# A convolution, attention and recurrence network on one core: the norm of the next image inside the last attention block, and a feed-forward in more steps

## The chip, the cores and the metric

The kernel runs on one core of one Trainium2 chip. Its metric is the device time of one execution in microseconds, given as the median of several runs. The engines that matter are TensorE (matmuls and transposes, PE in the profile, with PEld for its weight loads), VectorE (DVE), ScalarE (ACT), GpSimd (POOL), and SyncE (SP), which issues most of the transfers. Each engine works through its own queue in order.

## The reference, cut to what matters

The input is x of shape (4, 128, 64, 64): four images of 128 channels and 4096 positions. What is computed, in short:

```python
# layer 0
g = groupnorm(x, 32 groups)
e1, e2, asm = prelu(1x1 conv of g)            # 64, 64, 128 channels
x = x + softmax(e1^T e2) @ asm                # 4096 x 4096 scores per image
# layer 1, on tokens t (4096 x 128 per image)
a = layernorm(t)
q = running products of cos(a + rx)           # 16 heads of 8
a1 = layernorm(a + attention(q, q, q) @ w_comb.T + b_comb) * g1 + beta1
h  = relu((cos(a1[..., :8]) * cos(ry)) @ w1.T + b1)      # 512 wide
t  = t + layernorm(a1 + h @ w2.T + b2) * g2 + beta2
# last step, over all images
wx = batchnorm(layernorm(t) @ W.T)
y_t = sigmoid(wx_t + y_(t-1) @ V.T)           # along the positions
out = t + y
```

Here norms with no factors of their own are meant where none are written, and a1 is added again before the last norm of the attention layer.

## The kernel before, in words

The four images pass through two stages each. The first stage (`first_stage`, `layer0`) is the convolution attention: two convolutions of the normed image give e1 and e2 in four pieces of 1024 positions (`both_convs`, lines 373 to 387), a third gives asm, and then for each of eight chunks of 512 columns sixteen blocks of scores are multiplied on TensorE (`scores`, L439), exponentiated on ScalarE (L443), summed on VectorE (L451) and weighed on TensorE (L458). The second stage (`second_stage`, `attention`) is the attention over 16 heads, taken as eight pairs of heads with four blocks each. A block is a list of units (`order`, line 891). A unit multiplies scores (L948), exponentiates them (L960) and is weighed two units later (L801). Scores are symmetric, so "other" units, which lie off the diagonal, are also turned by VectorE (`run_flips`, L767) and multiplied a second time for the mirrored side (`mirror_step`, L780), sixteen steps for four units, into halves of one PSUM bank (`misc`); VectorE adds them up (L794). "Own" units on the diagonal need no turning. A last block has twelve other and four own units, in the order three other, one own. In the very last block of an image the exponentials go to a pool of six tiles, two for each unit, because the buffer of the image (`xs`) that otherwise serves as well is being loaded with the next image.

That load and the statistics of the next image's group norm are a generator (`prepare_image`, `norm_stats`, lines 333 and 1398). It is advanced once at the first unit of the last block and once at each of the units 6 to 13: one load and eight pieces of statistics (L337). The rest, two tiny matmuls (L342, L351) into the PSUM slot called `ps_tok` and a power on GpSimd (L241), is run after the last turning of the block. Then the next first stage begins with four of the eight normalisations (L363) and its convolutions.

The feed-forward of an image (`feed_forward`, line 1053) is done in eight groups of 512 tokens, and runs interleaved with the first stage of the next image; that of the fourth image runs alone at the end (`third_stage`). It is a generator too, with pauses (`yield`) between its steps. In the first stage `meanwhile` calls `step_late` once or twice after every weighed block, from the ninth call on; each call advances every living group by one step, and `in_steps(..., 14, 2)` starts a new group each 14 steps with at most two alive. The order of TensorE, ScalarE and VectorE in these stages follows the order in which the code issues the work; in `third_stage` a scheduler orders it. The steps that matter here: the projection of the attention (L1075), v and its statistics, the norm v on ScalarE (L283), the product with g1 and the sum with fb2 on GpSimd (L1083, L1084), the cosine, the 512 hidden values (L1120, L1129), the product back (L1137), u with its statistics and norm, the product with g2 and the sum with be2 on GpSimd (L1152, L1153), t2 on VectorE (L1158), its transposes (L291) and copy, its norm, transposes again, a copy to `last` (L1237), and the matmul for the batch norm's statistics (L1178, L1179). Matmuls of the feed-forward take turns on two PSUM banks (`ps_one`).

Of the kernel before, what the change touches and what calls it, by code (L numbers as in the profile page):

```python
# [26 lines left out]
def kernel(  # L27
# [32 lines left out]
    P = 128  # L60
# [19 lines left out]
    stats = ctx.enter_context(tc.tile_pool(name="stats", bufs=4))  # L80
# [252 lines left out]
    def norm_stats(n, xs):  # L333

        st = once.tile([P, NIC, 6], F32, tag="gst", name=f"gst{n}")
        for i in range(NIC):
            nc.vector.bn_stats(st[:, i, :], xs[:, ts(i, IC)])  # L337
            yield
        mv = once.tile([P, 2], F32, tag="gmv", name=f"gmv{n}")
        nc.vector.bn_aggr(mv, st)  # L340
        pg = get("ps_tok", f"pg{n}")
        nc.tensor.matmul(pg[:, 0:1], grp, mv[:, 0:1], start=True, stop=True)  # L342
# [5 lines left out]
        nc.vector.scalar_tensor_tensor(tv, dm, dm, mv[:, 1:2], ALU.mult, ALU.add)  # L348
        yield
        pv = get("ps_tok", f"pv{n}")  # L350
        nc.tensor.matmul(pv[:, 0:1], grp, tv, start=True, stop=True)  # L351
        yield gm, rsqrt(pv[:, 0:1], 1e-5, [P, 1], f"g{n}")

    def layer0(n, xs, xh, norm, shifted, begin, meanwhile):
# [118 lines left out]
        normalised(0, 4)  # L473
        both_convs(0)
        normalised(4, NIC)
# [164 lines left out]
    def attention(n, q, xs, tail, upcoming):  # L640
# [16 lines left out]
        misc = get("ps_misc", f"misc{n}")  # L657
        turns = []
# [271 lines left out]
        for pair in range(NPAIR):  # L930
            keys, queries, qa, later, denom = ready
            for b in range(NQB):
                block = {"acc": None}
                tiles = order(b)
                end_of_all = pair == NPAIR - 1 and b == NQB - 1

# [3 lines left out]
                for at, unit in enumerate(tiles):  # L940
# [75 lines left out]
                    if end_of_all and (at == 0 or 6 <= at < 6 + NIC):  # L1016
                        next(upcoming, None)
# [35 lines left out]
    def feed_forward(im, i, t2_rows, last, final):  # L1053
# [29 lines left out]
        nc.gpsimd.tensor_tensor(blocks(v), blocks(v), row4(g1_bc), ALU.mult)  # L1083
# [32 lines left out]
        for f0 in range(0, NF, 2):  # L1116
# [10 lines left out]
            for j in range(2):  # L1127
                bias = fb1_sb[:, f0 + j : f0 + j + 1]
                nc.scalar.activation(hs[-1][:, j, :], phs[j], AF.Relu, bias=bias)  # L1129
# [35 lines left out]
        nc.sync.dma_start(out=t2_rows[:, cols], in_=t2T)  # L1165
        norm(u, t2, factors)
# [3 lines left out]
        tokens_i = last(n, i, pt)  # L1170
        yield
# [10 lines left out]
    WsT = const.tile([P, P], F32, tag="WsT", name="WsT")  # L1182

    def fold_norm(W_sb):
# [88 lines left out]
    def first_stage(im, before):  # L1273
# [11 lines left out]
        with stage(f"conv{n}", **pools, **psum), tc.manual_schedule(engines=engines):  # L1285
            own, calls = [], [0]
            step_late = in_steps(feed_forwards(before) if before else [], 14, 2)
# [94 lines left out]
    def hold_every():  # L1382
# [3 lines left out]
        held["W"] = pool.tile([P, P], F32, tag="W_sb", name="W_sb")  # L1386
# [32 lines left out]
    with stage("fold", half=(HALF, 1), ps_one=(ONE, 1)):  # L1419
        fold_norm(held["W"])  # L1420
# [15 lines left out]
    with stage("runs", t2=((P, 2 * IC), 4 * N), half=(HALF, 2 * NS + 2), ps_one=(ONE, 2 * NS)):  # L1436
# [21 lines left out]
        def begin(k, t):  # L1458
# [3 lines left out]
                out_k, WsT, tokens_at(k, t), start=True, stop=t == -WARM, skip_group_check=True  # L1462
# [61 lines left out]
    with tc.If(any_bad > 0):  # L1524
# [5 lines left out]
        with stage(  # L1530
# [7 lines left out]
            W_again = half_tile("W_again")[:, 0:P]  # L1538
            nc.sync.dma_start(out=W_again, in_=W)
            fold_norm(W_again)  # L1540
# [90 lines left out]
```

## Time and profile before

| what | value |
|---|---|
| time before, median of 3 runs | 7238.97 us (7236.84 to 7239.09) |
| profiled execution, its time | 7238.09 us |
| profiled execution, its span | 7236.4 us |
| TensorE busy | 6893.3 us (95%) |
| VectorE busy | 5952.5 us (82%) |
| ScalarE busy | 6007.3 us (83%) |
| GpSimd busy | 2861.6 us (40%) |
| mean granted TensorE clock | 0.976 |

The span is what the profiler saw from the first instruction to the last; the run's own time is a little longer. First stages lie at about 25 to 415, 1665 to 2190, 3440 to 3960 and 5220 to 5740 us of the span, second stages between them, the last feed-forward at about 6982 to 7127 and the recurrence after it. A row of a timeline reads: start, duration, engine, line, operation, tile written <- tiles read, partitions x elements, count, and in brackets the idle time before it with what ended it. A row of waits reads: who waited <- for whom: total us, times, longest. A row of a stretch of time reads: from:to, its length, then the busy time of each engine with its count of instructions, the granted clock, the share of the DMA engines and GB/s.

### The profile page before, as it was taken

The page shows a single profiled execution, that of the slowest core. Times are in us where ns is not written, and L with a number is a line of the kernel's source. Part 1 is how long each engine was busy: PE and PEld are TensorE (multiplying, and loading weights), DVE is VectorE, ACT ScalarE, POOL GpSimd, SP SyncE. Part 2 cuts the span into 40 slices and gives each one's busy share as a digit, 9 for nine tenths or more (in the row PEclk, how much of TensorE's full clock was granted, in tenths as well). Part 3 has the DMA queues.
Part 4 walks back from the last instruction along what each step waited for, and adds up shares of the span by engine and source line. Part 5 has one row for each costly group of instructions (what it writes and reads, how often), then busy time and mean ns, then how long its engine had stood idle before and what let it go on. Part 6 is the DMA issues. An engine that isn't in the chain of part 4 may idle for free. (4 is left out here: it accounts for less than half of the span.)

```text
span 7236.4 us, 224777 instructions
## 1 busy us (share of the span) xinstructions
PE 6893.3 (95%) x92974; PEld 3741.7 (52%) x92974; DVE 5952.5 (82%) x7949; ACT 6007.3 (83%) x11919; POOL 2861.6 (40%) x10021
## 2 busy tenths in 40 slices
PE   8999999998989999999988999999998899999977
PEld 4545555555554555554554455555455455555546
DVE  5678899887768899889676998888867788898984
ACT  4479999995558999999455999999855599999976
POOL 0024444434323454443433354444433244444542
PEclk9999999999999999999998999999999999999988
DMA  1010000001111000000111100000011100000012
GB/s 38 30 39 25 29 20 21 21 9 35 38 43 40 27 22 20 22 23 20 30 38 44 37 22 20 21 25 21 23 32 36 44 33 22 22 26 27 11 60 106
DMA packets 85393, 221.20 MB, mean 31 GB/s; under 512 B 9490, under 2 KB 10644, under 8 KB 83588
## 3 DMA queue, kind: packets, MB, share of 16 engines
q1 hardware_dynamic: 79904, 195.10, 7.9%
q8 instruction: 731, 11.98, 0.7%
q10 hardware_dynamic: 4164, 11.41, 0.4%
q14 instruction: 306, 2.51, 0.1%
q0 software_dynamic: 288, 0.20, 0.0%
HBM read 141.63 MB, written 56.62 MB: 27 GB/s over the span
## 5 line engine op out<-in xcount | busy, mean ns | idle before, releaser
L960 ACT ACTIVATE e<-s 128x1024 f32<-128x1024 f32 (+1 forms) x3480 | 2949.1, 889 | 62.6 <-PE s L948 41.8
L767 DVE STREAM_TRANSPOSE t<-e 128x1024 f32<-128x1024 f32 x2240 | 2587.3, 1208 | 11.4 <-ACT e L960 9.1
L780 PEld LDWEIGHTS misc<-t,mirror 128*32 128x32 f32 x57344 | 1663.6, 110 | 1400.6 <-issue 1348.8
L780 PE MATMUL misc<-t,mirror 128*32 128x128 f32 x57344 | 1994.9, 273 | 20.6 <-DVE later L794 17.7
L960 ACT ACTIVATE xs<-s 128x1024 f32<-128x1024 f32 (+1 forms) x2152 | 1836.4, 894 | 44.6 <-PE s L948 31.5
L767 DVE STREAM_TRANSPOSE t<-xs 128x1024 f32<-128x1024 f32 x1344 | 1558.4, 1208 | 6.6 <-ACT xs L960 5.1
L801 PE MATMUL acc<-e,q_aug 128*32 128x512 f32 x11360 | 1523.7, 608 | 10.8 <-POOL q_aug L683 10.8
L948 PE MATMUL s<-queries,keys 32*128 32x512 f32 x9216 | 1219.7, 497 | 9.4 <-ACT e L960 3.4
L843 POOL COPY own<-o 32x36 f32<-32x36 f32 x2048 | 437.5, 214 | 1710.3 <-DVE o L835 1629.7
L458 PE MATMUL acc<-p,asmT 128*128 128x512 f32 x2048 | 952.5, 597 | 0.0
L801 PE MATMUL acc<-xs,q_aug 128*32 128x512 f32 x7072 | 942.2, 605 | 0.3 <-DVE o L835 0.3
L443 ACT ACTIVATE p<-s 128x1024 f32<-128x1024 f32 x512 | 499.5, 1022 | 468.3 <-PE s L439 452.2
L451 DVE TENSOR_TENSOR total<-total,p 128x1024 f32<-128x1024 f32 x448 | 572.8, 1279 | 326.6 <-ACT p L443 302.9
L948 PEld LDWEIGHTS s<-queries,keys 32*128 32x128 f32 x9216 | 480.2, 182 | 499.4 <-issue 380.0
L737 POOL COPY mirror<-q 32x128 f32<-32x128 f32 x2048 | 602.6, 294 | 237.9 <-PE misc L780 150.2
L868 POOL COPY other<-turned 32x64 f32<-32x64 f32 x1904 | 447.9, 235 | 628.2 <-DVE turned L858 549.6
L439 PE MATMUL s<-hl,e 128*128 128x512 f32 x2048 | 629.3, 452 | 44.9 <-ACT p L443 20.2
L960 ACT ACTIVATION_READ_ACCUMULATOR e<-s 128x1 f32 x2880 | 649.3, 225 | 0.0
L458 PEld LDWEIGHTS acc<-p,asmT 128*128 128x128 f32 x2048 | 386.7, 193 | 341.5 <-issue 317.3
L439 PEld LDWEIGHTS s<-hl,e 128*128 128x128 f32 x2048 | 406.7, 203 | 207.1 <-issue 100.0
L794 DVE TENSOR_TENSOR later<-later,misc 128x128 f32<-128x128 f32 (+1 forms) x576 | 162.7, 282 | 378.5 <-PE misc L780 375.3
L828 POOL COPY by_token<-by_key 32x4 f32<-32x4 f32 x2016 | 390.4, 194 | 85.3
(251 smaller groups left out, 4850.5 us busy)
## 6 DMA issues: line engine op xcount, KB each, us to landing
keys<-parts_dram SPq DMA_DIRECT2D x256, 256.0 KB
queries<-parts_dram SPq DMA_DIRECT2D x1024, 32.0 KB
fx<-x_dram SPq DMA_DIRECT2D x64, 256.0 KB
x_dram<-x SPq DMA_DIRECT2D x56, 256.0 KB
xs<-in_x_dram SPq DMA_DIRECT2D x16, 512.0 KB
t_dram<-t2T SPq DMA_DIRECT2D x32, 256.0 KB
t2s<-t_dram SPq DMA_DIRECT2D x16, 512.0 KB
parts_dram<-high SPq DMA_DIRECT2D x28, 256.0 KB
```

Of the source, the lines that this page charges most:

```text
L439: nc.tensor.matmul(s[:, j, :], stationary, moving, start=y == 0, stop=y == len(parts) - 1)
L443: nc.scalar.activation(p, s, AF.Exp)
L451: nc.vector.tensor_tensor(state[ic], state[ic], p, ALU.add)
L458: nc.tensor.matmul(state["acc", ic], asmT[:, ts(2 * jp + j, P)], p[:, j, :], start=jp == 0 and j == 0, stop=jp == NP - 1 and j == 1,)
L737: nc.gpsimd.tensor_copy(wv[ts(a, 32), s, :, :, ts(a, D)], own[ts(s, 32)])
L767: nc.vector.transpose(group["e"][h][:, k, :], es[h])
L780: nc.tensor.matmul(state["acc"][ts(2 * x + h, 32), :], state["w"][:, QT * (s // 4) + TG * x + s % 4, h, :], state["e"][h][:, :, ds(IC * x ...
L801: nc.tensor.matmul(it["in"]["acc"][ts(2 * h + x, 32), :], it["qa"][:, ds((2 * it["tiles"][x] + h) * V, 32)], it["e"][h][:, ts(x, IC)], sta ...
L843: nc.gpsimd.tensor_copy(own[ts(s, 32), ts(x, 4), h, :], ov[ts(2 * h + x, 32), s, :, 0:V])
L868: copy(to[ts(k, 32), h], tv[ts(2 * x + h, 32), k])
L948: nc.tensor.matmul(ss[h][:, x, :], keys[unit[x] // QT].bitcast(F32R)[r, ts(unit[x] % QT, P)], queries[b].bitcast(F32R)[r, :], start=True, ...
L960: nc.scalar.activation(es[h][:, ts(x, IC)] if split else es[h], ss[h][:, x, :] if split else ss[h].rearrange("p x c -> p (x c)"), AF.Exp, ...
```

## The change

In the last block of an image the order becomes all other units first and the own units last, and the generator of the next image is advanced at the first unit and at each of the last ten, which takes in its last two parts as well. For that the two tiny matmuls of the norm write into spare columns of the bank of the mirrored sums, which are set to zero at the start of the attention (`spare`), without the start flag. The first stage then normalises two pieces ahead of the first convolution and the other six between the first convolution and its activation. The rounding of the lower half of e2 goes from ScalarE to VectorE.

In the feed-forward the products with g1 and g2 go from GpSimd to VectorE, be2 is added to x0 on GpSimd ahead of time (x0's load moves up by two steps), and there are more pauses: between the norm v and the product with g1, before the norm u and after it, between the transposes of t2 and the norm of it, and before the last matmul; one before the product back now holds the addition to x0, one pair before t2 is gone. Three groups may be alive, and the pools follow: x1 from 2 to 3 buffers, fhalf from 6 to 8, stats from 4 to 6, mid from 8 to 7; the folded weights WsT move from the constants into a pool of the last stage.

```diff
-        pg = get("ps_tok", f"pg{n}")
-        nc.tensor.matmul(pg[:, 0:1], grp, mv[:, 0:1], start=True, stop=True)
+        pg = get("ps_norm", f"pg{n}")
+        alone = dict(start=n in (0, "r"), stop=True, skip_group_check=True)
+        nc.tensor.matmul(pg[:, 0:1], grp, mv[:, 0:1], **alone)
...
-        pv = get("ps_tok", f"pv{n}")
-        nc.tensor.matmul(pv[:, 0:1], grp, tv, start=True, stop=True)
+        pv = get("ps_norm", f"pv{n}")
+        nc.tensor.matmul(pv[:, 0:1], grp, tv, **alone)
...
             y, z = mid_tile(f"y{n}_{i}"), mid_tile(f"z{n}_{i}")
+            if i == 0:
+                normalised(2, NIC)
             prelu(pair(e1[:, cols]), pc, y, z, (b12_sb, minus_b12), a12_sb)
-            nc.scalar.copy(pair(e2[CR:P, cols]).bitcast(F32R), pair(e1[CR:P, cols]))
+            nc.vector.tensor_copy(pair(e2[CR:P, cols]).bitcast(F32R), pair(e1[CR:P, cols]))
...
-        normalised(0, 4)
+        normalised(0, 2)
         both_convs(0)
-        normalised(4, NIC)
...
         misc = get("ps_misc", f"misc{n}")
+        spare = [misc[:, ts(k, P)] for k in (2, 3)]
+        for t in spare:
+            nc.vector.memset(t[:, 0:1], 0.0)
+        here["ps_norm"] = lambda name: spare.pop(0)
...
-        def order(b):
+        def order(b, own_last):
...
+            if own_last:
+                return rest + own
             each = len(rest) // TG
             return [u for k in range(TG) for u in rest[each * k : each * (k + 1)] + own[k : k + 1]]
...
-                tiles = order(b)
                 end_of_all = pair == NPAIR - 1 and b == NQB - 1
+                tiles = order(b, end_of_all)
...
-                    if end_of_all and (at == 0 or 6 <= at < 6 + NIC):
+                    if end_of_all and (at == 0 or at >= len(tiles) - NIC - 2):
                         next(upcoming, None)
...
         norm(v, v, factors)
-        nc.gpsimd.tensor_tensor(blocks(v), blocks(v), row4(g1_bc), ALU.mult)
+        yield
+        nc.vector.tensor_tensor(blocks(v), blocks(v), row4(g1_bc), ALU.mult)
         nc.gpsimd.tensor_tensor(blocks(x1), blocks(v), row4(fb2_bc), ALU.add)
...
                 nc.scalar.activation(hs[-1][:, j, :], phs[j], AF.Relu, bias=bias)
+            if f0 == 0:
+                x0 = get("fhalf", f"fx0_{n}_{i}")
+                nc.sync.dma_start(out=x0, in_=im["x0"][:, cols])
             yield
-        yield
-        x0 = get("fhalf", f"fx0_{n}_{i}")
-        nc.sync.dma_start(out=x0, in_=im["x0"][:, cols])
+        nc.gpsimd.tensor_tensor(blocks(x0), blocks(x0), row4(be2_bc), ALU.add)
+        yield
         po = one_psum(f"pf{n}_{i}")
...
         factors = norm_factors(u, "u")
         yield
         yield
+        yield
         norm(u, u, factors)
-        nc.gpsimd.tensor_tensor(blocks(u), blocks(u), row4(g2_bc), ALU.mult)
-        nc.gpsimd.tensor_tensor(blocks(u), blocks(u), row4(be2_bc), ALU.add)
-        yield
-        yield
+        yield
+        nc.vector.tensor_tensor(blocks(u), blocks(u), row4(g2_bc), ALU.mult)
...
         nc.sync.dma_start(out=t2_rows[:, cols], in_=t2T)
+        yield
         norm(u, t2, factors)
         yield
         yield
         pt = transposed(blocks(u), f"pl{n}_{i}")
         tokens_i = last(n, i, pt)
+        yield
         yield
         if n != "r":
             token_products(n, i, tokens_i)
...
-        ffn = dict(x1=(HALF, 2), fhalf=(HALF, 6), hT=(MID, 2))
+        ffn = dict(x1=(HALF, 3), fhalf=(HALF, 8), hT=(MID, 2))
...
-        rest = dict(e=(BIG, 2), big=(BIG, 1), mid=(MID, 8))
+        rest = dict(e=(BIG, 2), big=(BIG, 1), mid=(MID, 7))
...
-            step_late = in_steps(feed_forwards(before) if before else [], 14, 2)
+            step_late = in_steps(feed_forwards(before) if before else [], 14, 3)
```

More of the change, by code (lines that the diff above doesn't have):

```diff
@@ L79 @@
     once = ctx.enter_context(tc.tile_pool(name="once", bufs=1))
-    stats = ctx.enter_context(tc.tile_pool(name="stats", bufs=4))
+    stats = ctx.enter_context(tc.tile_pool(name="stats", bufs=6))
     by_channel = ctx.enter_context(tc.tile_pool(name="by_channel", bufs=1))
@@ L1181, with fold_norm @@
     shift = const.tile([P, 1], F32, tag="shift", name="shift")
-    WsT = const.tile([P, P], F32, tag="WsT", name="WsT")
-    def fold_norm(W_sb):
+    def fold_norm(W_sb, WsT):
         bmv = once.tile([P, 2], F32, tag="bmv", name="bmv")
@@ L1284, in first_stage @@
         engines = {nc.tensor.engine, nc.scalar.engine, nc.vector.engine}
-        with stage(f"conv{n}", **pools, **psum), tc.manual_schedule(engines=engines):
+        others = {"ps_norm": lambda name: get("ps_tok", name)}
+        with stage(f"conv{n}", {}, others, **pools, **psum), tc.manual_schedule(engines=engines):
             own, calls = [], [0]
-            step_late = in_steps(feed_forwards(before) if before else [], 14, 2)
+            step_late = in_steps(feed_forwards(before) if before else [], 14, 3)
             def meanwhile(steps=1):
@@ L1385, in hold_every @@
         held["every"] = pool.tile([P, N, S], F32, tag="every", name="every")
-        held["W"] = pool.tile([P, P], F32, tag="W_sb", name="W_sb")
+        for name in ("W", "WsT"):
+            held[name] = pool.tile([P, P], F32, tag=name, name=f"{name}_sb")
         nc.gpsimd.dma_start(out=held["W"], in_=W)
@@ L1419 @@
     with stage("fold", half=(HALF, 1), ps_one=(ONE, 1)):
-        fold_norm(held["W"])
+        fold_norm(held["W"], held["WsT"])
     WARM, TOL = 16, 1e-6
@@ L1461, in begin @@
             nc.tensor.matmul(
-                out_k, WsT, tokens_at(k, t), start=True, stop=t == -WARM, skip_group_check=True
+                out_k, held["WsT"], tokens_at(k, t), start=True, stop=t == -WARM, skip_group_check=True
             )
@@ L1537 @@
                     token_products(n, i, every[:, n, ts(i, IC)])
-            W_again = half_tile("W_again")[:, 0:P]
+            pool, _ = here["big"]
+            W_again, WsT = (
+                pool.tile([P, P], F32, tag=name, name=f"{name}_again") for name in ("W", "WsT")
+            )
             nc.sync.dma_start(out=W_again, in_=W)
-            fold_norm(W_again)
+            fold_norm(W_again, WsT)
             with tc.For_i(0, S, SC) as s0:
```

## The prediction

> **What bounds the kernel now.** I read the page first (busy shares, slices), then the stretches of 100 us, then the waits of TensorE in one convolution stage, then the timelines at its worst gap and around the change of image.
>
> ```profile
> span 7236.4 us, 224777 instructions
> ...
> PE 6893.3 (95%) x92974; PEld 3741.7 (52%) x92974; DVE 5952.5 (82%) x7949; ACT 6007.3 (83%) x11919; POOL 2861.6 (40%) x10021
> ```
>
> ```profile
> 1900.00:2000.00 100.00, 91.81 (x359) 58.05 (x360) 77.35 (x163) 56.28 (x79) 37.11 (x42) 0.94 0.10 35
> 2000.00:2100.00 100.00, 86.09 (x358) 52.61 (x357) 64.58 (x150) 52.62 (x75) 28.27 (x32) 0.97 0.11 35
> ...
> 2400.00:2500.00 100.00, 99.89 (x1732) 50.45 (x1720) 88.94 (x91) 98.31 (x205) 35.93 (x146) 1.00 0.06 19
> ```
>
> The first is the page, the second the stretches, whose columns are busy us of PE, PEld, DVE, ACT, POOL, then the clock. TensorE sets the time: full in the attention stages (the row from 2400), 86 to 92 of 100 us in the three convolution stages that also carry a feed-forward (1700 to 2200 and its two likes). The five rows of 1700 to 2200 miss 51 us. The waits of TensorE from 1700 to 2215:
>
> ```profile
> PE pt L291 <- DVE t L1158: 14.3, 5, 5.3
> PE pwx L1178 <- ACT last L1237: 7.5, 3, 4.0
> PE acc L801 <- POOL q_aug L683: 5.6, 1, 5.6
> PE s L439 <- ACT p L443: 4.8, 2, 3.6
> PE pc L291 <- ACT hT L1129: 4.2, 7, 0.9
> PE pl L291 <- ACT q L283: 3.0, 1, 3.0
> ```
>
> They are steps of the feed-forward that were issued too close to what they read. At the longest, TensorE stands in front of the transposes of t2 (first line), while VectorE works without a pause and slowly:
>
> ```profile
> 1791.42 1.11 PE L291 MATMUL pt<-ident,t 128*128 128x128 f32 x4 [5.34 <-DVE t L1158]
> ```
>
> ```profile
> 1776.46 4.15 DVE L268 TENSOR_SCALAR x<-x,mv_t,r_t 128x128 f32<-128x128 f32 x4
> 1780.65 1.67 DVE L599 TENSOR_TENSOR arg<-x,rx_bc 128x512 f32<-128x512 f32 x1
> ```
>
> The four normalisations take 4.15 us where their mean of 422 ns makes 1.69, because GpSimd runs five 128x512 operations (L1067, L1083, L1084, L1152, L1153) from 1776.6 to 1783.5. Last, the change of image, TensorE's timeline and one row of VectorE's:
>
> ```profile
> 1662.16 0.38 PE L342 MATMUL pg<-gmv,grp 128*128 128x1 f32 x2 [2.55 <-DVE gmv L340]
> 1663.34 0.35 PE L351 MATMUL pv<-tv,grp 128*128 128x1 f32 x2 [0.79 <-DVE tv L348]
> ...
> 1682.64 3.75 PE L439 MATMUL s<-hl,e 128*128 128x512 f32 x8 [6.40 <-DVE hl L423]
> ```
>
> ```profile
> 1627.25 9.09 DVE L767 STREAM_TRANSPOSE t<-e 128x1024 f32<-128x1024 f32 x8
> ```
>
> The norm of the next image stands after the last block and opens gaps of 2.55 and 0.79 us; the 6.40 us later is the wait for the first scores' operands. Turning a tile costs 9.09 / 8 = 1.14 us.
>
> **What the Trainium skill says.** "SBUF — State Buffer", "Who interferes with whom": a VectorE tensor_tensor with both inputs in SBUF contends with GpSimd's reads, and a tensor_scalar in a two-port mode is shut out for a whole instruction. The trace agrees (4.15 against 1.69 us). "TensorE: Matmul & The Clock Gate", "Why this matters for your kernels": gaps over about 3 us drop the clock. It agrees: after the 5.34 us gap eight score matmuls take 3.76 us, not 2.39, and the next eight of L458 4.08, not 3.59, so that gap costs 1.9 us more. "PSUM — Partial Sum Buffer", "The four PSUM rules": a region set to zero and matmuls without the start flag may share a bank with other groups; so the norm may use the bank of the mirrored sums without a second bank. No row of before shows it; I price the two matmuls as now (0.38 and 0.35 us) and the memsets at under 0.2 us each, by the 0.09 us of the 128x32 memset (L221).
>
> **The change, part by part.**
>
> *The last block of an image.* Today its order is three other units, one own unit, and so on. Only the other units are turned by VectorE (two transposes, 2.27 us a unit; a unit takes TensorE 2.09 us, from the spacing of the L948 rows). Now twelve such units stand in a row, then four own ones. In this block the exponentials rotate in six tiles, three units, so ScalarE may fill unit u only when unit u-3 is turned. VectorE starts 4.64 us after the block's first score (1627.25 against 1622.61, behind L835). Its work to the end of the twelfth unit: 24 x 1.136 = 27.3, sums of L794 0.9, the wait before them 0.85, one turn of 0.4, and six pieces of norm statistics at 0.6: 33 us, so done 37.7 us after the first score, or 1660.3. The last two own units' exponentials (2 x 2.0 us) follow the start of that twelfth unit's second turning, 1659.2; the last also waits about 1 us for its scores, which queue on TensorE behind the first norm matmul. So the block ends near 1665, not 1659.6: 5 to 6 us later. In return the norm is ready, the 2.55 and 0.79 us gaps and the slow matmuls behind them (1.94 for 1.2, 1.86 for 0.6) fall away, and the first convolution is complete at 1671 instead of 1672.0. I take -1 us for each of three changes of image, between -7 (VectorE keeps up) and +4. The fourth image has no statistics there: its block ends 2.6 us later.
>
> *First pieces and rounding.* Two normalisations ahead rather than four: nothing, since the first matmul starts after one piece (25.20 against 24.60). The six then sit in the 2.2 us of ScalarE and the mirrored matmuls. The rounding moves from ScalarE (1.04 us) to VectorE (about 0.9, twice L422's 0.43). ScalarE no longer holds the second piece's rounding in front of the first exponential: today it ends at 42.5, then comes a table load of 1.28, and TensorE waits 2.24 and 1.16 us for that exponential. I take -2.5 us in the first stage and -1 in each of three others (0.70 and 1.16 there): -5.5.
>
> *The feed-forward in the convolution stage, per stage.* Counting its pieces between pauses: 27 become 30, a new group still starts every 14 steps, so a third is alive in two steps of 14 and all eight end at step 128 of 135. Issue order is nearly the old one. (a) The last product (7.5) gets two steps for one, both norms of ScalarE three steps after their statistics for two: of 7.5 + 3.0 + 4.8 = 15.3 us I take away 12. (b) The two multiplications leave GpSimd (1.39 and 1.38 us, 0.69 each on VectorE by L1147), the addition of be2 goes ahead onto x0. Two of five GpSimd operations leave the pile-up above, which gives VectorE back about what the products cost it (2/5 of its 4.2 us loss against 1.38), and t2 no longer has two GpSimd operations before it: of 14.3 I take away 5, since VectorE's queue, not GpSimd, ends this wait. (c) New: now the last product, two hidden matmuls and the next group's projection follow each other in one step, seven times a stage, on two one-bank buffers (the built order of TensorE shows the row). The second hidden matmul waits for the statistics (0.70 us, L1179) behind what VectorE has in its queue, the projection for the first relu (0.68): 1.3 us each, +9; at least 0.4, at most the 5.3 seen at t2. (d) The clock after the long gaps that go: -5. Sum: -13 a stage, -39 in three. The x0 load moves two steps ahead in SP's queue, and its addition (1.5 us, L1153) stands in GpSimd's queue two steps, some 8 us, behind it; were the load late, the powers of the norms would queue behind it and ScalarE's norms behind these; the one step more covers that. The pool mid keeps seven buffers for eight: an exponential is read by both readers within some four of its turns, so this is free, and so are the larger pools and WsT's new place.
>
> *The feed-forward after the last image.* GpSimd is busy almost without a pause from 7005 to 7047 and 7058 to 7114; ScalarE waits for its factors. 8 x 2.77 = 22 us of products leave it. The middle, 7051 to 7090, is TensorE's (eight times 5 us) and stays. After it today's tail runs to 7124; the chain of the last group alone (sum 0.7, two statistics 3.6, two factors 3.0, two norms 3.3, two products 1.4, transposes, copy and last matmul 2.8, last statistics 0.7) is 15.5 us, so it could end at 7106; with the queues on ScalarE I take 7113. The part before gains 3. -14, and +2.6 from the late block: -11, between -3 and -19.
>
> Sum: -3 - 5.5 - 39 - 11 = -58.5. I keep 51 of it, since the freed gaps seldom close whole: a span of 7185; the profiled execution took 7238.09 for its 7236.4, 1 us under the median, so **7188 us**.
>
> **The rivals.** *The convolution stage gives nothing back*: the seven new meetings cost what the wider steps save. For: VectorE is at 65 to 77% there and comes late already at t2; against: TensorE's wait for the statistics was 0.6 us at the most. -20: 7219. *Everything closes*: VectorE keeps up in the last block, and of each stage's 51 us 30 go. -90 - 21 - 5 - 14 = -130: 7109, and half of the way 7150; against it stand the transposes' sum and the bursts on VectorE. *Slower*: VectorE becomes the bound in the convolution stage: it takes 8 x 1.38 + 4 x 0.9 = 15 us more a stage and every one of the 21 meetings waits as t2 does now, 5.3 us: +111 against -51 - 27 = -78 without the meetings, so +33, 7272; it decides from 78 / 21 = 3.7 us a meeting, and measurably from 4.4. *The change does nothing to speak of*: the steps fall beside other bursts and the sum is within 14 us.
>
> **How the numbers follow.** The forecast 0.50, nothing from the stages 0.22, everything 0.14, slower 0.10, no effect 0.04 (near 7235). Within 0.2% (14.5 us, about what a measurement of this kernel tells from no change) lie the last and half of the second: 0.15; slower 0.10; faster 0.50 + 0.14 + 0.11 = 0.75. Range 7150 to 7230: above lie the slower case and most of no effect (0.13), below half of "everything" (0.07); the forecast's own is 7165 to 7212.
>
> **What would show it.** The TensorE row of 1700 to 2200: 51 us missing becomes about 38. The waits of pt for t near 9, of pwx for last near 1; a new one of ph for wx_stats near 5 or more. Around the last block: ScalarE waiting for t (L767's like) and no gap at the norm. The distance from the last score to the end shrinks by 11. Wrong if the wait for wx_stats exceeds 25 us a stage, or if the last block loses over 8 us.

## The result, and the profile after

The changed kernel takes 7196.88 us (median of five runs, 7193.35 to 7199.95) against 7236.84 us for the kernel before in the same comparison: a ratio of 0.9944, 95% interval 0.993 to 0.9959, 40 us faster. The forecast was 7188 with a range of 7150 to 7230, so side and range held. The way there did not: two large errors of opposite sign met in the sum. The profiled execution took 7196.66 us for its span of 7194.9.

The page after, its span and busy shares:

```profile
span 7194.9 us, 224876 instructions
...
PE 6875.7 (96%) x92974; PEld 3726.6 (52%) x92974; DVE 5958.0 (83%) x8037; ACT 5994.8 (83%) x11903; POOL 2783.9 (39%) x9957
```

TensorE has as many instructions as before, is busy for 17.6 us less and idle for 24 us less. Where these 41.4 us lie follows from the starts and ends of TensorE's rows in both timelines. (The stretches leave out some 7 us between the convolution stages and the attention stages behind them, the same in both kernels.) A "last block" is the one that the change reorders; "first score" of a convolution stage is its first L439 row (L442 after).

| stretch | before, us | after, us | difference | the prediction |
|---|---|---|---|---|
| start to the first attention score of image 1 | 420.3 | 416.6 | -3.6 | -2.5 |
| three convolution stages with a feed-forward, first score to last weighed block | 1512.1 | 1475.8 | -36.4 | -39, and -3 of the rounding |
| four attention stages up to their last block | 4820.4 | 4810.0 | -10.4 | nothing |
| three last blocks, from their first score to the next stage's first score | 182.4 | 196.9 | +14.5 | -3 |
| fourth image's last block, to its last weighing | 35.8 | 40.4 | +4.6 | +2.6 |
| from there to the end | 258.7 | 248.3 | -10.3 | -14 |

A convolution stage first. The stretch of 100 us that answers to the first shown of before (busy us of PE, PEld, DVE, ACT, POOL, then the clock):

```profile
1900.00:2000.00 100.00, 89.74 (x363) 55.43 (x361) 75.04 (x168) 60.90 (x85) 27.55 (x37) 0.97 0.12 40
```

TensorE is short of 10.3 us in this hundred, more than the 8.2 us of before, so a single hundred doesn't show the gain. The same stage whole, from first score to last weighed block, before and then after:

```profile
1682.64:2186.56 503.92, 457.24 (x1780) 281.75 (x1781) 351.82 (x726) 267.48 (x361) 166.38 (x231) 0.95 0.12 38
```

```profile
1681.23:2173.00 491.77, 448.55 (x1780) 275.02 (x1781) 349.80 (x745) 266.59 (x358) 167.23 (x255) 0.96 0.12 38
```

The stage is 12.15 us shorter. TensorE runs the same 1780 matmuls in 8.7 us less, at a higher granted clock, and its idle time falls only from 46.7 to 43.2 us. Most of the gain is faster matmuls, not closed gaps; in the other two stages TensorE is busy 8.3 and 7.3 us less. The row of 1700 to 2200 misses 44 us, where the prediction expected about 38. TensorE's waits after, from 1681 to 2174 (who waits <- for whom: total us, times, longest):

```profile
PE pt L291 <- DVE t L1168: 15.0, 5, 6.0
PE pz L291 <- DVE zs L1114: 8.0, 4, 3.5
PE pl L291 <- ACT q L283: 6.4, 1, 6.4
...
PE ph L1129 <- DVE wx_stats L1191: 3.4, 6, 0.6
PE s L442 <- ACT p L446: 1.1, 1, 1.1
PE pw L1083 <- DVE wx_stats L1191: 1.0, 1, 1.0
```

Of those shown of before, the 7.5 us of pwx for last and most of the 4.8 us of s for p are gone. The wait for t is as long as it was (14.3), that of pl for q has doubled, and pz waits 8.0 us for zs where it waited 2.7. The longest gap of before, at t2, has moved to another group and is longer:

```profile
1985.30 1.12 PE L291 MATMUL pt<-ident,t 128*128 128x128 f32 x4 [6.01 <-DVE t L1168]
```

VectorE's timeline shows what t stands behind there:

```profile
1975.83 2.80 DVE L622 TENSOR_TENSOR q<-q,r 128x64 f32<-128x64 f32 x3
...
1980.27 2.78 DVE L454 TENSOR_TENSOR total<-total,p 128x1024 f32<-128x1024 f32 x2
1982.98 0.88 DVE L622 TENSOR_TENSOR q<-q,r 128x64 f32<-128x64 f32 x3
1983.77 0.68 DVE L1165 TENSOR_TENSOR q<-q,g_bc 128x512 f32<-128x512 f32 x1
1984.55 0.69 DVE L1168 TENSOR_TENSOR t<-q,fx 128x512 f32<-128x512 f32 x1
```

The two operations of GpSimd directly in front of t are gone, and t waits all the same: behind the sums of the scores and other work in VectorE's own queue. GpSimd still has a part in it. The first row, three products of 128x64, takes 2.80 us while GpSimd computes two of its sums (L1075 and L1093, 1975.64 to 1978.19); three more of the same shape take 0.88 us a little later.

The change of image, TensorE's timeline after:

```profile
1656.74 0.38 PE L343 MATMUL misc<-gmv,grp 128*128 128x1 f32 x2 [1.27 <-DVE gmv L340]
...
1662.18 1.12 PE L379 MATMUL pc<-q,w_sb 128*128 128x512 f32 x2
1666.46 3.70 PE L786 MATMUL misc<-t,mirror 128*32 128x128 f32 x128 [3.16 <-DVE later L800]
```

Of the two gaps at the norm the first is smaller (1.27 for 2.55) and the second gone (the norm's second matmul follows at 1659.14 without a wait), but a new one of 3.16 us stands behind the first half of the first convolution's first piece: the last mirrored steps wait for `later`, and the second half of that piece stands behind them. In the block itself ScalarE waits for turned tiles, as forecast:

```profile
1646.24 0.60 ACT L968 ACTIVATE e<-s 128x512 f32<-128x512 f32 x1 [2.80 <-DVE t L773]
```

and the wait for `later` is explained by VectorE's timeline and then GpSimd's of the same microseconds:

```profile
1660.39 4.77 DVE L364 TENSOR_SCALAR q<-xs,gm,r_g 128x512 f32<-128x512 f32 x4 [0.67 <-POOL r_g L241]
1665.07 0.71 DVE L841 STREAM_TRANSPOSE o<-acc 128x512 f32<-128x512 f32 x1
1665.71 0.50 DVE L364 TENSOR_SCALAR q<-xs,gm,r_g 128x512 f32<-128x512 f32 x1
1666.13 0.28 DVE L800 TENSOR_TENSOR later<-later,misc 128x128 f32<-128x128 f32 x1
```

```profile
1660.32 4.09 POOL L1075 TENSOR_TENSOR fx<-fx,bc_bc 128x512 f32<-128x512 f32 x3
```

Four normalisations take 4.77 us: the first three 1.50, 1.49 and 1.48, the fourth, when GpSimd has stopped, 0.54. GpSimd computes the first line of the feed-forward for three groups at once there.

### The profile page after: what moved, and what is told of

The parts are those of the page before. It is cut to its first block, busy times and chain, and to the rows that moved or that the text cites. A ratio compares the mean times of both kernels' runs of the same rounds, so it can differ in the third digit from the quotient of the medians.

```text
span 7194.9 us, 224876 instructions
## 1 busy us (share of the span) xinstructions
PE 6875.7 (96%) x92974; PEld 3726.6 (52%) x92974; DVE 5958.0 (83%) x8037; ACT 5994.8 (83%) x11903; POOL 2783.9 (39%) x9957
## 5 line engine op out<-in xcount | busy, mean ns | idle before, releaser
L442 PE MATMUL s<-hl,e 128*128 128x512 f32 x2048 | 608.7, 440 | 29.5 <-DVE hl L426 22.8
L442 PEld LDWEIGHTS s<-hl,e 128*128 128x128 f32 x2048 | 393.2, 196 | 184.4 <-issue 98.9
```

Of the source, the lines that this page charges most:

```text
L442: nc.tensor.matmul(s[:, j, :], stationary, moving, start=y == 0, stop=y == len(parts) - 1)
```

## The experiments

Times are medians, with the ratio to the kernel before and its 95% interval. Single runs of a kernel lie up to some 10 us apart, so what belongs to one stretch is read from the profiles and only the whole from the medians.

### The parts alone

**The old last block in the changed kernel.**

```diff
-                tiles = order(b, end_of_all)
+                tiles = order(b, False)
...
-                    if end_of_all and (at == 0 or at >= len(tiles) - NIC - 2):
+                    if end_of_all and (at == 0 or 6 <= at < 6 + NIC):
```

> The changed kernel with the order of the last block and the advance of the norm's generator put back as before (three other units, one own unit; statistics at units 6 to 13, the norm finished after the block); everything else stays changed. Theory A: the new last block is a loss. From the first score of the last block to the first score of the next image's convolution stage the changed kernel takes 4.1, 4.5 and 5.9 us more than before, and the fourth image's last block 4.6 us more; so this kernel gives about 19 us back: span near 7176, and those stretches return to 60 to 61 us. Rival B: the stretches grew because the head of the convolution (six normalisations moved, rounding on VectorE) got worse, and the order is innocent: then they stay at 64 to 67 us and the span near 7195.

Measured: 7180.84 us, ratio 0.9921 (0.9904 to 0.9938), 16 us less than the changed kernel. The three stretches from the last block to the first score take 60.8, 59.7 and 61.0 us, the fourth block 35.8. The new last block is a loss (A).

**The last-block part alone on the kernel before** (its order, the generator's advance, the spare columns, two and six normalisations).

> The kernel before with the last-block part alone: own units last, the norm inside the block and in the spare columns, two and six normalisations; rounding and feed-forward as before. Theory A: slower than before by 14.5 + 4.6 = 19 us, span near 7255; ScalarE waits for VectorE's turning in the last block. Rival B (what the prediction said of this part: -1 us for each change of image and +2.6): span near 7236. If the parts add up, this loss and the gain of the first run are the same size.

Measured: 7254.5 us, 1.0023 (1.0014 to 1.0033), 17.5 us slower than before. The stretches take 65.4, 66.8 and 63.5 us, the fourth block 41.6. Theory A again.

**The feed-forward part alone on the kernel before** (all hunks of the feed-forward, its pools, WsT).

> The kernel before with the feed-forward part alone: steps, products on VectorE, be2 on x0, three groups, pools. Theory A: the whole gain comes from here: -36 in the three convolution stages, -10 in the last feed-forward, -10 at the start of the attention stages: span near 7180, faster than the changed kernel. Rival B: the rounding and the last block carry part of it, so that this kernel lies between 7200 and 7220. The first stage (no feed-forward in it) should take as long as before, 378.3 us, since its gain of 3 us belongs to the rounding.

Measured: 7192.23 us, 0.9937 (0.9921 to 0.9954), 45 us faster than before. The convolution stages take 496.3, 494.9 and 495.0 us, the last stretch 247.2, the first stage 379.5 (378.3 before). Both readings were off: the part carries more than the whole gain, but less than A's 57 us, and the stages are 2.5 to 4.5 us longer than in the changed kernel.

**The rounding alone on the kernel before.**

```diff
-            nc.scalar.copy(pair(e2[CR:P, cols]).bitcast(F32R), pair(e1[CR:P, cols]))
+            nc.vector.tensor_copy(pair(e2[CR:P, cols]).bitcast(F32R), pair(e1[CR:P, cols]))
```

> The kernel before with the rounding of e2 on VectorE and nothing else. The prediction: 2.5 us in the first stage and 1 us in each of the other three, 5.5 in all: 7231. Theory A (from the runs so far: the first stage is 3 to 4.6 us shorter wherever the rounding is on VectorE, 374 to 376 us for 378.3 to 379.6): 4 us in the first stage and 1 to 2 in the others, 7228 to 7230. Rival B: the first stage's gain belongs to the two normalisations made ahead instead of four, not to the rounding: the first stage stays at 378 and the time at 7236.

Measured: 7226.35 us, 0.9984 (0.9978 to 0.9991), 10 us faster. The first stage takes 375.3 us for 378.3, and the gap of 2.24 us in front of the third convolution is gone. TensorE's timeline of the kernel before, then of this one:

```profile
44.89 0.73 PE L393 MATMUL pa<-ba_rows,ones 128*128 128x512 f32 x2 [2.24 <-ACT p L443]
```

```profile
42.16 1.05 PE L393 MATMUL pa<-ba_rows,ones 128*128 128x512 f32 x2
```

Theory A had the place; the size is above its upper end. The three parts sum to +17.5 - 44.8 - 10.3 = -37.6, the change gave -40.0: within the scatter of these times they add.

### The last block: order, norm, or a collision

**Old order, norm inside the block** (only `order(b, False)` in the changed kernel).

> The changed kernel with the old order of the last block (three other, one own) but the norm still finished inside the block (generator advanced at the last ten units). It tells the order from the place of the norm. Theory A1: only the order costs, because twelve turned units stand in a row with six exponential tiles; then the block ends about 37 us after its first score for 44, the gaps of 2.6 and 0.8 us at the norm are gone as well, and the span is near 7170, better than the run with the whole old last block by about 3 x 2 us. Theory A2: the norm's statistics among the last turns delay VectorE by their 5 us in either order; then the block ends near 42 us and the span lies near 7185. Rival B: 7195.

Measured: 7194.28 us, 0.9941 (0.9924 to 0.9958). The block of the first image ends 46.3 us after its first score and the next first score comes at 67.0, 65.3 and 66.9. A1 falls: the norm's place costs as much without the new order. A2 falls too: it had the statistics delay VectorE and the block end near 42 us. The time is that of B. TensorE's timeline of this kernel shows the reason:

```profile
1656.57 0.59 PE L343 MATMUL misc<-gmv,grp 128*128 128x1 f32 x2 [6.52 <-DVE gmv L340]
```

In the old order TensorE is ahead of VectorE by 6.5 us at this point, and it waits, although a unit of scores stands behind the matmul in its queue.

**New order, norm after the block** (only the generator's line as before).

> The changed kernel with its own-units-last order, but with the norm's statistics at units 6 to 13 and the rest of the norm after the block, as before. With the runs so far (old order and norm after: 60.0 to 61.1 us from the block's first score to the next stage's first score; old order and norm inside: 65 to 67; new order and norm inside: 64 to 67) it fills the square. Theory A: the order alone costs what the fourth image's block shows, +4.6 (block end at 41.6 for 37.0), and the norm's gaps after it stay or shrink by no more than 3: first score at 62 to 65. Rival B: the order is free, and what costs is the norm inside the block: block end at 38 or less and first score at 60 or less.

Measured: 7191.16 us, 0.9937 (0.9921 to 0.9952). The block ends at 42.3 us, near A, but the first score comes at 61.0, 61.1 and 61.1, below A and above B. Neither theory holds. For three images the order alone is free by the time of the first score; only the fourth block keeps its 4.6 us. The median lies 10 us above that of the old last block (7180.84), but the two profiled executions have the same span within 0.1 us; what the medians have beyond the fourth block is not placed. The square, in us from the block's first score to the next first score:

| | norm after the block | norm inside |
|---|---|---|
| old order | 60.8, 59.7, 61.0 | 67.0, 65.3, 66.9 |
| new order | 61.0, 61.1, 61.1 | 64.2, 65.7, 67.0 |

What doesn't move explains it. The statistics are complete, and the norm's first matmul can start, 39.6 us after the block's first score in the kernel before (1662.16 - 1622.61), 39.7 in the changed kernel (1656.74 - 1617.06) and 39.5 in the two with the old order. With the new order alone they are complete at 39.6 as well, and the matmul, which stands behind the block there, follows at 42.2 without a wait. VectorE has the same turns and statistics to do in each, one after the other; neither of the two orders and neither place of the norm brings that moment forward. Putting the matmul ahead of work that TensorE could do meanwhile can then only delay this work.

**The sum of x1 on VectorE**, the last block as in the changed kernel.

```diff
-        nc.gpsimd.tensor_tensor(blocks(x1), blocks(x1), row4(bc_bc), ALU.add)
+        nc.vector.tensor_tensor(blocks(x1), blocks(x1), row4(bc_bc), ALU.add)
```

> The changed kernel, untouched in its last block, with one line moved: the sum of x1 and the projection's bias (the first line of the feed-forward) goes from GpSimd to VectorE. In the changed kernel three of these sums (1.28 to 1.46 us each) run on GpSimd exactly while the first three normalisations run on VectorE, and these take 1.50, 1.49 and 1.48 us for the 0.50 to 0.58 of the others; the sums of the mirrored side stand behind them on VectorE and the last mirrored steps on TensorE behind those (a wait of 3.16 us). Theory A: that collision is what the norm inside the block costs beyond the longer block; without it the normalisations take 0.55 us each and the first score comes 3 us earlier, at 61 to 63 us after the block's first score for 64.2 to 67.0: 9 to 12 us in three, 7185 to 7188. Rival B: the order on VectorE alone makes the loss (normalisations ahead of the sums): less than 3 us in all, 7194 or more.

Measured: 7175.37 us, 0.9916 (0.9899 to 0.9932), 21.5 us less than the changed kernel. VectorE's timeline and TensorE's at the place of the collision:

```profile
1660.01 1.92 DVE L364 TENSOR_SCALAR q<-xs,gm,r_g 128x512 f32<-128x512 f32 x4 [0.67 <-POOL r_g L241]
```

```profile
1663.23 3.70 PE L786 MATMUL misc<-t,mirror 128*32 128x128 f32 x128 [0.30 <-DVE later L800]
```

Four normalisations in 1.92 us for 4.77, a wait of 0.30 us for 3.16, and the first scores at 61.3, 61.4 and 61.4. That takes back 12.8 of the 14.5 us lost there: the collision is shown (A). The shorter wait makes 8.6 of them in three changes. The rest is the clock behind the gap: in the changed kernel the 128 mirrored matmuls after it take 3.70, 5.21 and 6.38 us at the three changes, at a granted clock of 1.00, 0.70 and 0.57, though the gap is 3.15 to 3.16 us each time; with the sum moved they take 3.70 us at all three. The convolution stages gain 2.2 to 2.6 us each and the last stretch 4.0 besides, which the expectation didn't have; the longest wait for t in the stage shown falls from 6.01 to 5.24 us.

**The convolution ahead of the mirrored steps** (old last block).

```diff
-                nc.tensor.matmul(
-                    pc[:, j, :], w12_sb, xh[:, ts(2 * i + j, IC)], start=True, stop=True
-                )
+                with tc.high_priority(offset=600) if i == 0 and n != "r" else ExitStack():
+                    nc.tensor.matmul(
+                        pc[:, j, :], w12_sb, xh[:, ts(2 * i + j, IC)], start=True, stop=True
+                    )
...
-        normalised(0, 2)
+        with tc.high_priority(offset=600) if n != "r" else ExitStack():
+            normalised(0, 2)
```

> The changed kernel with the old last block, and the first two normalisations and both halves of the first convolution's first piece pulled ahead of the last sixteen mirrored steps on TensorE (they get a higher priority in the scheduler). In all traces so far the second half stands behind these 128 small matmuls (4.4 us), and ScalarE sits idle for 14.9 us until it is done. Theory A: the way to the first scores (activation, rounding, difference, transfer, operands) starts 4.3 us earlier and nothing else is late: the first score comes 56 us after the last block's first score for 60.8, three times, so about 13 us: 7168. Rival B: the mirrored steps, pushed back, delay the sums behind them and the scores wait as long as now: 7181.

Measured: 7184.47 us, 0.9924 (0.991 to 0.9937): nothing gained over 7180.84. First scores at 62.4, 61.1 and 62.4. A falls; the time is near B's, but not through late sums. The convolution was done at 1663.93, and ScalarE's timeline shows its activation waiting for the mirrored steps:

```profile
1669.29 1.11 ACT L324 ACTIVATE y<-pc,b_sb 128x1024 f32<-128x1024 f32 x1 [16.48 <-PE misc L788]
```

**The same with the pool mid placed first.**

```diff
-        pools = {**ffn, **sums, **rest}
+        pools = dict(mid=rest.pop("mid"), **ffn, **sums, **rest)
```

> The run before with the convolution ahead of the mirrored steps gained nothing: its convolution was done 5 us earlier, but ScalarE's first activation still waited for the last mirrored step, 16.48 us idle. Theory A: its output tile lies (pool mid, the last one placed) where the turned tiles of the attention lie, so it must wait until the mirrored steps have read them. This kernel is that one with the pool mid placed first, over the attention's queries: the activation then starts within 1 us of the convolution's end, about 4 us earlier, and the first scores come 4 to 5 us earlier three times, 12 us: near 7170. Rival B: the activation waits for the mirrored steps for another reason (PSUM, or TensorE's order), or another tile laid elsewhere waits in its place: 7180 to 7185.

Measured: 7266.13 us, 1.004 (1.0025 to 1.0054), slower than before. ScalarE's timeline:

```profile
1668.55 1.12 ACT L324 ACTIVATE y<-pc,b_sb 128x1024 f32<-128x1024 f32 x1 [11.22 <-PE pc L380]
1680.17 1.11 ACT L325 ACTIVATE z<-pc,minus_b 128x1024 f32<-128x1024 f32 x1 [10.51 <-POOL own L878]
```

The first activation now starts when the convolution ends (1664.76 + 3.75 = 1668.51), so it was the place of its tile that held it, as A has it, but A's gain didn't come. But z, the next tile of the pool, now lies where GpSimd still gathers the attention's results, and waits 10.51 us for them; the first scores come 84 to 88 us after the block's first (B's last clause). Another layout wasn't tried, so whether 4 us a change can be had is open.

### The feed-forward: products and groups

**Two groups alive** (old last block).

```diff
-            step_late = in_steps(feed_forwards(before) if before else [], 14, 3)
+            step_late = in_steps(feed_forwards(before) if before else [], 14, 2)
```

> The changed kernel with the old last block, and at most two groups of the feed-forward alive instead of three, so that a group starts every 14 or 16 steps and the row of last product, two hidden matmuls and next projection in one step falls apart for every second group. Theory A: these meetings cost little (the waits of hidden matmuls and projection for the statistics sum to 4.4 us a stage), so the stages gain at most 3 us each and the third group is not what made them shorter: 7172 to 7184. Rival B: the third group matters, since all eight groups must end before the scores do; the last group then runs alone after the scores and the stages grow by 5 us or more each: 7195 or more.

Measured: 7268.28 us, 1.0042 (1.0027 to 1.0058), slower than before by 31 us. Its second convolution stage in two stretches, from the first score to the last weighed block and from there to the first attention score (columns as above):

```profile
1677.09:2136.66 459.57, 425.97 (x1666) 259.83 (x1666) 333.80 (x675) 242.41 (x317) 138.49 (x196) 0.97 0.11 34
2136.66:2197.09 60.43, 29.75 (x138) 20.10 (x137) 19.99 (x78) 21.28 (x40) 20.24 (x45) 0.68 0.09 31
```

Groups of thirty steps with two alive aren't through when the scores are: 60 us of feed-forward remain, with TensorE busy for half of them at a clock of 0.68. Together 520 us for the 494 of the kernel with three groups (B). So the added steps pay only with a third group. (The third group with the old, shorter steps wasn't run.)

**The products back on GpSimd** (old last block).

```diff
-        nc.vector.tensor_tensor(blocks(v), blocks(v), row4(g1_bc), ALU.mult)
+        nc.gpsimd.tensor_tensor(blocks(v), blocks(v), row4(g1_bc), ALU.mult)
...
-        nc.vector.tensor_tensor(blocks(u), blocks(u), row4(g2_bc), ALU.mult)
+        nc.gpsimd.tensor_tensor(blocks(u), blocks(u), row4(g2_bc), ALU.mult)
```

> The changed kernel with the old last block (as in the first run, 7180.8 us) and with the two products, with g1 and with g2, given back to GpSimd; the steps, be2 on x0 and the three groups stay. The prediction took 5 us off TensorE's wait for t2 in each convolution stage because two of five GpSimd operations leave, but the changed kernel still waits 15.0 us there (14.3 before). Theory A: the place of the products doesn't matter in the convolution stages (491 to 494 us each, within 2), TensorE's wait for t stays within 2 us of 15, and only the last feed-forward loses, by 5 to 10 us: 7186 to 7191. Rival B: the products' place is worth the predicted 5 us a stage and the stages without it are longer: 497 to 499 us each, 7200 or more.

Measured: 7198.2 us, 0.9946 (0.993 to 0.9961), 17 us more than with the products on VectorE. The stages take 494.6, 495.3 and 494.9 us for 494.3, 491.7 and 494.4, so 1.5 us each on average; the last stretch takes 257.5 for 249.0; the profiled executions differ by 7.9 us in span. TensorE's wait for t is 11.3 us, shorter than with the products on VectorE (15.0). The mechanism of A holds (the place matters little in the stages, 8.5 us in the last feed-forward), but the median lies above A's range; the profiled execution lies at the low end of this kernel's runs (7194.1) and the compared one at the high end of its own (7186.2), and what the medians have beyond the profiles is not placed.

### Both findings together

The old last block and the sum of x1 on VectorE, the two edits shown above.

> The changed kernel with the old last block (7180.8 us in the first run) and the sum of x1 on VectorE (7175.4 us with the new last block). Theory A: with the old last block nothing collides with the normalisations (0.5 us each there), so the moved sum gains nothing at the change of image, but it keeps what it gave elsewhere, 7 us in the three convolution stages (489.5 us each) and 4 us in the last feed-forward; and the old block spares the 5 us of the fourth image and about 0.5 us at each change: span near 7168, time near 7170. Rival B: the gain in the stages came from a shifted start, not from the sum's place, and the two don't add: 7175 to 7181.

Measured: 7168.31 us, 0.9907 (0.989 to 0.9923), 28.6 us less than the changed kernel and the lowest time of all kernels here. Stages of 489.1, 489.0 and 490.4 us, a last stretch of 245.2, first scores at 61.1, 61.1 and 60.7: as A has it.

## Why the prediction was right, and where it was wrong

**The last block.** The first half of the step holds. VectorE was through with the twelfth unit 37.6 us after the first score (37.7 forecast), ScalarE waited for it, and the block ended at 44.3 for the forecast 42 to 43; the two matmuls in the bank of the mirrored sums took 0.38 us each, as priced. The step that failed is "in return the norm is ready ... and the first convolution is complete at 1671 instead of 1672.0". In its own clock (from the block's first score) the convolution's first piece was complete at 54.1 us instead of 48.4. The prediction gave the normalisations no more time than before and forgot that what follows the norm on VectorE, the sums of the mirrored side, holds TensorE's last mirrored steps, and with them the second half of the convolution. It also didn't look at which GpSimd work the same moment releases. The three stretches grew by 14.5 us where -3 was forecast, and 12.8 of them are the collision that the moved sum removes. What the trace of before could have told: VectorE, not TensorE, sets when the norm is known. Even without the collision the new block comes to 61.3 to 61.4 us, no better than the old one. The prediction had named "if the last block loses over 8 us" as a sign of being wrong; over the three changes, for which it had forecast -3, this sign came true, and the total held in spite of it.

**The rounding.** Right in place and kind, too small: -5.5 forecast, -10 measured (6.5 to 16 by its interval). The profile of the rounding alone has 7.6 us of it in the forecast places: 3.5 up to the first attention score, 2.0 at the changes of image, 2.1 in the three stages. The rounding took 0.69 us on VectorE, not 0.9. Two normalisations ahead instead of four cost nothing, as taken: the first stage takes 375.3 us with four (rounding alone) and 375.2 with two (the changed kernel).

**The convolution stages.** -39 forecast for the feed-forward, -36.4 measured with some 2 us of the rounding in it, and right by cancellation. (a) The longer steps were to take 12 of 15.3 us of waits; the three came to 7.5 (0 + 6.4 + 1.1), so 7.8. One of them, the norm's q, became longer. (b) "Of 14.3 I take away 5" is wrong: 15.0 remain, and with the products on GpSimd the wait is 11.3. GpSimd's share of VectorE's trouble was taken as proportional to its count of operations, but t stands behind VectorE's own queue, which now has the products in it, and the sum of x1, which stayed on GpSimd, still slows that queue: with it moved the waits for t sum to 13.2 us. Nobody priced zs, which waits 5.3 us more. (c) The new meetings exist, but they cost 3.4 + 1.0 = 4.4 us a stage, not 9; this is the row of one of them in TensorE's timeline:

```profile
1863.16 0.50 PE L1129 MATMUL ph<-zT,f_sb 128*128 128x512 f32 x1 [0.56 <-DVE wx_stats L1191]
```

Most of these waits are 0.56 us, near the lower bound of 0.4, so the slower rival, which needed 3.7 us at each, was far off. (d) The clock was to give 5 us; the same matmuls are busy 8.7 us less. Before, TensorE worked 44.4 us of this stage at a granted clock of 0.50, in ten stretches, and after 29.6 us in seven. If full speed halves such time, 7.4 of the 8.7 us are the clock; this is an estimate from these two figures. "TensorE: Matmul & The Clock Gate", "Why this matters for your kernels", in the Trainium skill, warns of gaps above some 3 us. The trace agrees in part: each such gap of this stage, five before and four after, has a slow stretch with it, but slow stretches also follow gaps of 2.09 and 2.13 us before and of 2.19 and 1.99 us after. The prediction counted this term last, and it is about as large as what (a) gave. The third group, "alive in two steps of 14", was given no price at all; with these steps the stage takes 26 us more without it. No run parts the added pauses from one another or from the addition of be2.

**What no step had.** The four attention stages up to their last blocks are 10.4 us shorter in sum, 7.0 of them in the second and the fourth. There the page shows TensorE waiting 10.8 us, in two waits, for `q_aug` (L801) in the kernel before and not at all after. The wait is gone in every run with the feed-forward part, with the products on GpSimd too, and stays with the rounding alone, where the two stages still take 1206 us. With two groups it is gone as well, but there TensorE waits for queries and keys in its place and the two stages take 1207 us. So the wait ends with the steps or the addition of be2, which no run parts; the 3.4 us of the other two stages have no cause shown.

**The last feed-forward.** -14 and +2.6 forecast, -10.3 and +4.6 measured. The tail is what shrank: the wait of pwx for the last norm's output fell from 17.5 us in eight waits before (L1178) to this, a row of TensorE's waits in that stretch after:

```profile
PE pwx L1190 <- ACT every L1248: 5.5, 6, 2.2
```

With the products back on GpSimd 8.5 of these 10 us return, so the relief of GpSimd is the cause of most of it, as argued.

**The sum.** The steps gave -58.5; the span moved by -41.4. The three last blocks came out 17.5 us worse, the convolution stages with their share of the rounding 5.6, the fourth block 2 and the last stretch 4; the attention stages came out 10.4 better and the first stretch 1. The cut to -51 for gaps that "seldom close whole" happened to cover part of an error made elsewhere.

## What to carry to other kernels

Before work is moved to an earlier moment, find which engine sets that moment (here VectorE, 39.6 us after the block's first score, in every version) and list what the moment releases on all engines, GpSimd included, because they will run at once. A pipeline of thirty steps that starts a group every fourteen needs three groups alive (30 / 14, rounded up), or its tail runs alone after the cover has ended. Where an instruction waits for something that it doesn't read, look at what lay in its output's memory.

## What was not expected of the hardware

"SBUF — State Buffer", "Who interferes with whom", in the Trainium skill, says that a tensor_scalar in a two-port mode and a GpSimd instruction shut each other out for a whole instruction. The runs agree, though they don't show in which mode this tensor_scalar works, and add the price of a run of them: three normalisations of 128x512 (0.54 us alone) and three GpSimd sums of 128x512 (1.28 to 1.46 us) took turns, and each normalisation took 1.48 to 1.50 us. GpSimd's copies of 32x36 beside the same normalisation cost nothing that shows (0.53 to 0.58 us with the order alone). Moving that single sum, 1.27 us on GpSimd and 0.68 us on VectorE, 32 times in the program, was worth 21.5 us.
